# Two graph layers on one core: first scores behind the plain block, weight sums in an order of their own, three token tiles lent out

## Chip, cores, metric

One core of one Trainium2 chip. The metric is the device time of one execution of the whole kernel, in microseconds (us); a run gives one number, and the median of several runs is compared. TensorE is PE in the profile (its weight load PEld), VectorE is DVE, ScalarE is ACT, GpSimd is POOL, SyncE is SP.

## What is computed

The input x is 128 graphs of 64 nodes with 768 features, with an adjacency matrix for each graph. x is normalised and passed through relu, and goes through two layers of the following; the result is added to x.

```
m_left  = h @ W_left.T                     # 768 x 768
m_right = h @ W_right.T
u = (h m_left.T) on and above the diagonal, (h m_right.T) below it, / sqrt(768)
attention = exp(u) * adj, each row divided by its sum
h = relu(layer_norm(attention @ (h @ W_lin.T + b)))
```

## The kernel before

Layers are numbered l = 0 and 1 in the code (layer one is l = 0). Each layer has a first pass (pass_one: the scores and the attention) and a second pass (pass_two: the rest). Tokens are cut into 32 parts of 256 (4 graphs each), each a tile "ht" of 128 x (6 x 256). The work below is that of pass_one.

**Products.** For a part, m_left and m_right together are 2 x 3 x 3 blocks of 256 x 256 x 256, so 18 weight blocks ("raw", values 0 to 17). They are not multiplied one by one, but by a fast scheme: 40 products (PRODUCTS), each of one *weight form* and one *token form*, serve three parts at once. Weight forms are sums of raw blocks, made once a layer: W_OPS lists 101 sums (values 18 to 118), 50 of them without a factor other than 1 on the first operand; only those can go to POOL, the others go to DVE. Token forms are sums of the nine token blocks of three parts: T_OPS lists 38 (values 9 to 46), made anew for each block of three parts, on POOL, always in the order of T_OPS. READS says to which of the 18 outputs each product is added: the first addition to an output is a copy on ACT, the others are adds on DVE, from PSUM into the tiles M.

**Order.** `put(slot, f)` writes work into a plan; `turn_of(slot)` runs what stands there, two slots a product. Each engine works its own queue in order, so the slot fixes only the order of what each queue gets. Layer one begins with a **plain block** (`order`, L877 on): parts 0 and 1 by the 18 raw blocks, 12 chains of 3 products each, 36 products or 72 slots; each chain's bank is copied into M by ACT (L889). So there is time to make weight sums. Then `for k in ...` goes over blocks of three parts with 40 products each: k = 1 begins at slot 72 and k = 2 at slot 152. The **scores** of block k-1 (`scores`, L733, small matmuls of tokens by M) stand behind product 3 of block k, and the softmax of these scores (`chain`, wm on POOL first, L745) is put 10 slots behind the start of the block.

**Weight sums.** `Weights` holds which value lies in which of 51 tiles g (REG). `some(eng, reach)` (L531) takes the first of the next 10 (POOL: 40) sums whose operands are there, DVE preferring those with a factor. On DVE an operand is copied by ACT into a PSUM bank first (`stage`, L517) and read from there. `turn_of` counts 0.62 us a DVE sum and 1.35 us a POOL sum against the slot's time, plus the time of what `timed` marks on DVE; ScalarE's work is not counted. POOL gets weight sums in slots 8 to 59. `need(v)` gives out a sum, on DVE, if a product needs it and it isn't there yet.

**Token sums.** `Tokens.step` gives one to POOL if the parts are ready (`ready`), if fewer than 11 token tiles are out (LIMIT) and if a tile is free; it takes the one that has been free longest.

**Preparing parts.** `prepare(b, slot)` makes parts 2b and 2b+1 from rows of x, one step a slot: four statistics on DVE (L336), one square root on ACT and the scales on DVE, four norms on ACT (L412), four transposes on DVE (L465), the store to DRAM (L461, SP). Three slots later SP loads the part in its new layout (L368), and 16 slots after that it counts as ready. The rows of the next block are asked for at the end of this one (behind block 2: 8 slots later, slot 53). Block 1 is prepared from slot 16, block 2 from 30 and block 3 from 60. Blocks 1 and 2 give parts 2 to 5; k = 1 uses parts 2, 3 and 4.

## Time and profile before

| | us |
|---|---|
| median of 3 runs | 2648.96 (2647.83 to 2654.08) |
| the profiled execution | 2648.42 |
| its span, first to last instruction | 2646.6 |
| TensorE busy | 2591.6 |
| VectorE busy | 1780.6 |
| GpSimd busy | 1763.1 |
| ScalarE busy | 935.4 |

A row of a timeline gives the start of a group of instructions from the span's start, its length, the engine, the line in the kernel, the operation, out<-in by the program's names, shapes and the count; in brackets stands how long the engine had been idle before, and what ended that. Where a helper issues the instruction its line is the helper's: L245 is every add of two tiles, L522 an add with a factor. A float32 matmul appears as two, so a product has 8 and a chain 24.

### The profile page before, as it was taken

Reading aid. Unit: us, or ns where it says so; the run is one execution under the profiler, and the core shown is the slowest. Engines: PE = TensorE matmul, PEld = TensorE weight load, DVE = VectorE, ACT = ScalarE, POOL = GpSimd, SP = SyncE. Lnnn points to the kernel's source line nnn. Section 1 sums busy time; section 2 is a strip of 40 time slices with the busy share of each in tenths; the row PEclk is TensorE's granted clock in tenths of the full one; section 3 lists DMA queues with packets and bytes.
Section 4 is the critical chain, followed back from the end, with each engine's and each line's share of the span. In section 5 each row is a group of like instructions: output and inputs, shape, how many; then the busy total and the mean of one; then the engine's idle time right before and its main releaser. Section 6 shows DMA issues by size and latency. Waiting matters only on the chain. (4 is left out here: it accounts for less than half of the span.)

```text
span 2646.6 us, 47202 instructions
## 1 busy us (share of the span) xinstructions
PE 2591.6 (98%) x18122; PEld 2217.1 (84%) x18122; DVE 1780.6 (67%) x2888; ACT 935.4 (35%) x1969; POOL 1763.1 (67%) x1392
## 2 busy tenths in 40 slices
PE   9899999999999999999999999999999989999998
PEld 8788888888888888888798888888888878887886
DVE  7878787777768445554456667677666676666667
ACT  5522223223113244454542222122222335555453
POOL 4766676666668657676276666667666657878786
PEclk9999999999999999999999999999999999999999
DMA  7443534343421354445794424253532215555655
GB/s 220 113 111 86 124 93 110 93 119 79 98 60 56 123 156 149 159 139 182 219 282 101 121 68 108 71 129 93 136 98 70 67 49 157 157 167 166 177 161 146
DMA packets 258465, 331.84 MB, mean 125 GB/s; under 512 B 56002, under 2 KB 190402, under 8 KB 258242
## 3 DMA queue, kind: packets, MB, share of 16 engines
q1 hardware_dynamic: 241442, 320.56, 44.3%
q10 hardware_dynamic: 16800, 8.26, 1.2%
q8 instruction: 145, 2.38, 0.4%
q14 instruction: 78, 0.64, 0.1%
HBM read 213.39 MB, written 115.34 MB: 124 GB/s over the span
## 5 line engine op out<-in xcount | busy, mean ns | idle before, releaser
L245 POOL TENSOR_TENSOR g<-ht 128x512 f32<-128x512 f32 (+1 forms) x620 | 785.9, 1279 | 420.8 <-PE Z L702 71.6
L245 POOL TENSOR_TENSOR g<-g,g 128x512 f32<-128x512 f32 (+1 forms) x310 | 397.9, 1291 | 136.7 <-PE C L702 22.0
L245 POOL TENSOR_TENSOR g<-ht,g 128x512 f32<-128x512 f32 (+1 forms) x272 | 346.1, 1282 | 164.8 <-PE Z L702 42.8
L702 PE MATMUL X<-g,g 128*128 128x256 f32 (+1 forms) x1080 | 252.9, 377 | 6.0 <-DVE m L914 6.0
L1006 PE MATMUL Z<-g,g 128*128 128x256 f32 x1024 | 244.1, 380 | 3.5 <-ACT hl L300 3.2
L702 PE MATMUL C<-g,g 128*128 128x256 f32 x1008 | 239.7, 381 | 4.9 <-POOL g L245 2.2
L702 PEld LDWEIGHTS X<-g,g 128*128 128x128 f32 x1080 | 203.0, 191 | 34.8 <-DVE m L914 6.8
L702 PE MATMUL Y<-g,g 128*128 128x256 f32 (+1 forms) x968 | 225.7, 376 | 3.8 <-POOL g L245 3.8
L1006 PEld LDWEIGHTS Z<-g,g 128*128 128x128 f32 x1024 | 191.6, 190 | 35.8 <-issue 4.1
L379 ACT ACTIVATE ht<-ht,b_col,a_col 128x256 f32<-128x256 f32 x384 | 196.1, 591 | 69.0 <-DMA ht<-h 53.8
L702 PEld LDWEIGHTS C<-g,g 128*128 128x128 f32 x1008 | 190.5, 190 | 32.9 <-POOL g L245 3.5
L702 PE MATMUL Z<-g,g 128*128 128x256 f32 (+1 forms) x936 | 217.0, 375 | 0.0
L702 PE MATMUL D<-g,g 128*128 128x256 f32 x880 | 209.8, 381 | 1.8 <-POOL g L245 1.8
L702 PEld LDWEIGHTS Y<-g,g 128*128 128x128 f32 x968 | 182.0, 190 | 27.8 <-POOL g L245 4.2
L702 PE MATMUL V<-g,g 128*128 128x256 f32 (+1 forms) x840 | 194.6, 375 | 3.1 <-POOL g L245 1.6
L702 PEld LDWEIGHTS Z<-g,g 128*128 128x128 f32 x936 | 174.5, 190 | 23.1
L702 PEld LDWEIGHTS D<-g,g 128*128 128x128 f32 x880 | 168.1, 191 | 25.7 <-POOL g L245 2.5
L1006 PE MATMUL X<-g,g 128*128 128x256 f32 x768 | 182.7, 379 | 0.0
L702 PEld LDWEIGHTS V<-g,g 128*128 128x128 f32 x840 | 157.6, 191 | 23.3 <-POOL g L245 1.7
L1206 POOL TENSOR_TENSOR z<-z,b 128x768 f32<-128x768 f32 x62 | 112.7, 1829 | 81.7 <-DVE z L1203 77.2
L245 DVE TENSOR_TENSOR m<-m,Y 128x512 f32<-128x512 f32 (+2 forms) x196 | 126.5, 667 | 58.4 <-ACT m L910 35.7
L245 DVE TENSOR_TENSOR m<-m,D 128x512 f32<-128x512 f32 x180 | 118.2, 677 | 70.0 <-ACT m L910 51.3
(222 smaller groups left out, 4612.0 us busy)
## 6 DMA issues: line engine op xcount, KB each, us to landing
ht<-h SPq DMA_DIRECT2D x126, 768.0 KB, 6.3
h<-xb SPq DMA_DIRECT2D x124, 384.0 KB, 6.6
z<-z SPq DMA_DIRECT2D x128, 192.0 KB, 3.1
x<-z SPq DMA_DIRECT2D x128, 192.0 KB, 5.4
xr<-in_x_dram SPq DMA_DIRECT2D x120, 192.0 KB, 3.8
out_dram<-xr SPq DMA_DIRECT2D x120, 192.0 KB, 2.7
x<-in_x_dram SPq DMA_DIRECT2D x112, 192.0 KB, 5.4
g<-form SPq DMA_DIRECT2D x40, 256.0 KB, 5.6
```

The source lines that it names most:

```text
L245: (eng.tensor_add if sign == "+" else eng.tensor_sub)(o, a, b)
L379: nc.scalar.activation(ht, ht, AF.Relu, bias=cols[1][:, c:c + 1], scale=cols[0][:, c:c + 1])
L702: nc.tensor.matmul(o, w[:, c, g * P:(g + 1) * P], t, start=(new and g == c == at == 0), stop=(c == K2 - 1), skip_group_check=True)
L1006: nc.tensor.matmul(p[:, n], b[t][:, c, r * P:(r + 1) * P], w[s][:, c, :], start=(i in FIRST and i not in PRELOAD and n == c == 0), stop=(c ...
L1206: nc.gpsimd.tensor_add(zs[k], zs[k], rows["b"])
```

## The change

- **Scores.** In layer one the scores of parts 0 and 1 stand directly behind the plain block, ahead of product 0 of block 1; the products are then read one by one from the first on. Their softmax is put 2 slots behind the start of the block in place of 10.
- **Weight sums.** They are given out from a list of their own, START_OPS. `turn_of` keeps clocks for VectorE, ScalarE and GpSimd, which also count norms, copies and the wait of the scales. `some` works out when each of the next 10 (POOL: 20) sums could begin, by its operands, its tile and its engine, and takes the first that could begin within 0.7 us of the earliest. VectorE may be given work up to 0.5 us ahead (behind slot 72: 3.5 us). POOL gets sums from slot 0 to 59. The bank of the scores is no staging bank from chain 10 on; two staging banks stay in use in block 1.
- **Tiles.** A tile is chosen by the time at which its last planned use ends, for weight sums and for token sums. While weight sums are left, 9 token tiles may be out, and from slot 60 on a weight sum leaves one tile free. Part 5's place lends three tiles to token sums that are dead by product 20, and the places of parts 0 and 1 lend six more behind their scores; all go back at slot 113, when parts 5, 6 and 7 are loaded.
- **Slots.** Block 1 is prepared from slot 19, block 2 from 31; block 3's parts count as ready 16 slots behind the load in place of 22.

The numbers of matmuls, token sums, weight sums and reads stay as they are.

```diff
+    clock = {"vector": 0.0, "scalar": 0.0, "pool": 0.0}
-    def timed(us, f):
-        f.vector = us
+    def timed(f, *steps):
+        f.steps = steps
         return f
+    def passes(f):
+        for e, us in getattr(f, "steps", ()):
+            clock[e] += us
...
+    START_OPS = (
+        4, 27, 14, 0, 3, 2, 1, 9, 29, 6, 7, 12, 26, 15, 36, 8, 80, 10, 30, 11, 83, 81, 68, 5, 16, 56, 31, 39, 85,
...
     class Weights:
         def take(self):
             of = max(self.extra, free, key=len)
-            return of.popleft() if of else None
+            if not of:
+                return None
+            t = min(of, key=lambda t: busy.get(id(t), 0))
+            of.remove(t)
+            return t
+        def begins(self, eng, op):
+            dead = self.dead(op)
+            t = self.at[dead] if dead is not None else min(self.extra or free or (None,), key=lambda t: busy.get(id(t), 0))
+            x, y = (self.made.get(s, 0) for s in (op[1], op[3]))
+            at = max(y, self.until.get(id(t), 0), clock[NAMES[eng]])
+            if self.stage and eng is nc.vector:
+                x = max(x, clock["scalar"], self.until.get(id(self.stage[0]), 0)) + 0.6
+            return max(x, at)
         def emit(self, eng, op):
+            if dead is None and len(free) <= self.spare:
+                return False
+            us = 1.3 if eng is nc.gpsimd or not self.stage else 0.65
+            end = clock[NAMES[eng]] = self.made[v] = at + us
...
+        def some(self, eng, reach, now):
+            ops = [(max(self.begins(eng, op), now) + (0.4 if eng is nc.vector and op[2] == 1 else 0), n, op)
+                   for n, op in enumerate(self.left[:reach])
+                   if op[1] in self.at and op[3] in self.at and (eng is nc.vector or op[2] == 1)
+                   and (len(free) > self.spare or self.dead(op) is not None)]
+            if not ops:
+                return False
+            soon = min(ops)[0] + 0.7
+            at, _, op = next(o for o in ops if o[0] <= soon)
+            return at <= now + 4.5 and self.emit(eng, op)
...
     class Tokens:
         def emit(self, eng):
             v, a, b, sign = self.queue.pop(0)
-            t = free.popleft()
-            self.out += 1
+            if self.own and self.last[v] < SOON:
+                t = self.own.popleft()
+            else:
+                t = min(free, key=lambda t: busy.get(id(t), 0))
+                free.remove(t)
+                self.out += 1
...
     def pass_one(l, start, final):
-            weights, tokens = Weights(() if l else W_OPS, 2, True), TOKENS[l]
+            weights, tokens = Weights([] if l else [W_OPS[i] for i in START_OPS], 2, True), TOKENS[l]
             def turn_of(slot):
+                now = slot * 0.87 if l == 0 or slot >= 80 else slot * 0.6 + 20.8
+                if slot == start["tokens"]:
+                    weights.spare = 1
+                for e in clock:
+                    clock[e] = max(clock[e], now - 0.5)
...
-                    while clock["vector"] <= now and weights.some(nc.vector):
-                        clock["vector"] += 0.62
+                    while clock["vector"] <= now + (3.5 if slot > 2 * PLAIN else 0.5) and weights.some(nc.vector, 10, now):
+                        pass
+                    if slot < start["tokens"]:
+                        while clock["pool"] <= now + 0.5 and weights.some(nc.gpsimd, 20, now):
+                            pass
+                tokens.limit = Tokens.LIMIT - 2 * bool(weights.left)
+            def lend(*ps):
+                views = [HT[1, 0, p][:, j * K2:(j + 1) * K2, :] for p in ps for j in range(3)]
+                tokens.own.extend(views)
+                tokens.mine.update(id(t) for t in views)
+            if l == 0:
+                for p in range(2, 6):
+                    HT[1, 0, p] = big.tile([P, C, TH], F32, name="ht", bufs=6)
+                lend(5)
+                def back():
+                    assert len(tokens.own) == 9
+                    tokens.own.clear()
+                    load_part(1, 0, 5)
+                put(begins(1) + 2 * SOON + 1, back)
...
-                    lag = 22 if b > 2 else 30 if l else 16
+                    lag = 22 if b > 3 - l else 30 if l and b < 3 else 16
+                    if l == 0 and 5 <= p < 8:
+                        at = begins(1) + 2 * SOON + p - 4
...
+                if n == 10:
+                    weights.stage = [KEEP["Z"], KEEP["V"]]
...
-            weights.stage = []
+            weights.stage = [] if l else [KEEP["Z"], KEEP["V"]]
+            if not l:
+                scores(0)
+                lend(0, 1)
...
-                    put_all(slot + 2 * SCORED + 4, softmax(k - 1), 3)
+                    put_all(slot + (2 * SCORED + 4 if l or k > 1 else 2), softmax(k - 1), 3)
...
-                    if i == SCORED and k:
+                    if i == SCORED and l + k > 1:
                         scores(k - 1)
-                    if i >= SCORED or k == 0:
+                    if i >= SCORED or l + k < 2:
...
-    pass_one(0, {"weights": 0, "pool": 8, "tokens": 60, 1: 16, 2: 30}, final_of(0))
+    pass_one(0, {"weights": 0, "tokens": 60, 1: 19, 2: 31}, final_of(0))
```

More of the change, by code (lines that the diff above doesn't have):

```diff
@@ L474, in places @@
             pool.tile(shape, F32, name=n, bufs=bufs)
+    busy = {}
+    NAMES = {nc.vector: "vector", nc.gpsimd: "pool"}
     class Weights:
@@ L491, in __init__ @@
             self.extra = deque(extra)
+            self.made, self.until, self.spare = {}, busy, 0
         def used(self, v):
@@ L509, in emit @@
                 return False
+            us = 1.3 if eng is nc.gpsimd or not self.stage else 0.65
+            end = clock[NAMES[eng]] = self.made[v] = at + us
+            if self.stage and eng is nc.vector:
+                bank = self.stage.pop(0)
+                self.stage.append(bank)
+                clock["scalar"] = max(self.made.get(a, 0), clock["scalar"], self.until.get(id(bank), 0)) + 0.6
+                self.until[id(bank)] = end
+                bank = bank.rearrange("p (c d) -> p c d", c=K2)
+                nc.scalar.copy(bank, x)
+                x = bank
+            for s in (a, b):
+                self.until[id(self.at[s])] = max(self.until.get(id(self.at[s]), 0), end)
+            self.until[id(t)] = end
             if dead is not None:
@@ L592, in __init__ @@
             self.count = {}
+            first = {t: i for i, (_, t) in reversed(list(enumerate(PRODUCTS)))}
+            for v, a, b, _ in reversed(T_OPS):
+                for s in (a, b):
+                    first[s] = min(first.get(s, 99), first[v])
+            self.last = {v: max([i for i, (_, t) in enumerate(PRODUCTS) if t == v] +
+                                [first[o] for o, *ab, _ in T_OPS if v in ab]) for v, *_ in T_OPS}
+            self.own, self.mine, self.limit = deque(), set(), self.LIMIT
         def value(self, k, v, cut=False):
@@ L610, in step @@
         def step(self, slot, eng=None):
-            if self.k >= len(SUPER) or slot < self.ready.get(self.k, 10 ** 9) or self.out >= self.LIMIT or not free:
+            if self.k >= len(SUPER) or slot < self.ready.get(self.k, 10 ** 9) or self.out >= self.limit or not free:
                 return False
@@ L631, in used @@
             if v >= 9 and n == self.uses[v]:
-                free.append(self.at.pop((k, v)))
-                self.out -= 1
+                t = self.at.pop((k, v))
+                (self.own if id(t) in self.mine else free).append(t)
+                self.out -= id(t) not in self.mine
         def need(self, k, v):
```

58 lines of the change are left out of this document (30 added, 28 removed), and 3 rows, old and new, of the table START_OPS.

## The prediction

> **What bounds the kernel now.** I read the page's busy times first, then the busy time by stretch, then TensorE's instructions in order of time, and then the queue of each engine that releases them.
>
> ```profile
> span 2646.6 us, 47202 instructions
> PE 2591.6 (98%) x18122; PEld 2217.1 (84%) x18122; DVE 1780.6 (67%) x2888; ACT 935.4 (35%) x1969; POOL 1763.1 (67%) x1392
> ```
>
> TensorE is busy for 2591.6 of 2646.6 us. The change takes no matmul away, so it can win only idle or slow TensorE time, and 55.0 us of idle time are left in the whole span. By stretches of 25 us the only large hole of the first 150 us is here (columns: PE, PEld, DVE, ACT, POOL busy, granted clock, DMA share, GB/s):
>
> ```profile
> 75.00:100.00 25.00, 16.29 (x226) 12.98 (x227) 20.44 (x35) 14.97 (x28) 19.34 (x17) 0.80 0.49 124
> 80.00:85.00 5.00, 3.61 (x9) 2.90 (x10) 4.79 (x9) 4.95 (x10) 3.18 (x3) 0.50 1.03 200
> ```
>
> TensorE's rows show that this is the seam between the plain block and layer one's first 40 products (start, length, what; in brackets the idle time before):
>
> ```profile
> 17.75 5.35 PE L702 MATMUL D<-ht,g 128*128 128x256 f32 x24
> ...
> 69.55 5.34 PE L702 MATMUL Y<-ht,g 128*128 128x256 f32 x24
> 77.08 2.51 PE L702 MATMUL C<-g,g 128*128 128x256 f32 x8 [2.19 <-POOL g L245]
> 81.39 3.78 PE L702 MATMUL D<-g,g 128*128 128x256 f32 x8 [1.79 <-POOL g L245]
> 84.96 2.03 PE L702 MATMUL X<-g,g 128*128 128x256 f32 x8
> 90.80 2.57 PE L702 MATMUL Y<-g,g 128*128 128x256 f32 x8 [3.80 <-POOL g L245]
> 93.30 5.16 PE L733 MATMUL sc<-m,ht 128*32 128x95 f32 x192
> 99.49 1.97 PE L702 MATMUL C<-g,g 128*128 128x256 f32 x8 [1.04 <-ACT m L910]
> 101.30 1.89 PE L702 MATMUL D<-g,g 128*128 128x256 f32 x8
> ...
> 160.00 1.89 PE L702 MATMUL Y<-g,g 128*128 128x256 f32 x8
> 168.73 4.60 PE L733 MATMUL sc<-m,ht 128*32 128x95 f32 x211
> ```
>
> The ten chains from 17.75 to 69.55 lie 5.18 us apart, so the plain block would be over at 74.73. From product 5 (101.30; I count from 0) to product 39 (160.00) are 34 products, 1.7265 us each, without a gap: after the seam nothing waits. The later scores need 4.60/211 = 21.8 ns a matmul, so 192 cost 4.19 us; at 93.30 they took 5.16. Without any wait and at full clock product 4 would start at 74.73 + 4 x 1.7265 + 4.19 = 85.83. It started at 99.49. **The seam costs 13.66 us**, and that is what can be won. Every wait but the last names POOL, so I looked at POOL's queue, and at those behind it.
>
> ```profile
> 69.47 6.33 POOL L245 TENSOR_TENSOR g<-g,g 128x512 f32<-128x512 f32 x5 [5.95 <-ACT Z L517]
> 75.76 2.50 POOL L245 TENSOR_TENSOR g<-ht 128x512 f32<-128x512 f32 x2
> 78.72 1.27 POOL L245 TENSOR_TENSOR g<-ht 128x512 f32<-128x512 f32 x1 [0.45 <-DMA ht<-h]
> 83.09 2.51 POOL L245 TENSOR_TENSOR g<-ht 128x512 f32<-128x512 f32 x2 [1.75 <-DVE g L522]
> 88.13 2.61 POOL L245 TENSOR_TENSOR g<-ht,g 128x512 f32<-128x512 f32 x2 [2.53 <-DVE g L522]
> 97.26 1.43 POOL L745 TENSOR_TENSOR wm<-adj,tri 128x256 f32<-128x256 f32 x2
> 108.51 1.28 POOL L245 TENSOR_TENSOR g<-g,g 128x512 f32<-128x512 f32 x1 [0.52 <-PE C L702]
> ```
>
> Token sums are given in the fixed order of T_OPS. Values 9 and 10 run at 75.76, value 11 waits for token part 4 until 78.72, 13 and 15 wait for DVE to let go of a tile, and 16, which product 3 needs, ends at 90.74: product 3 starts at 90.80. So tokens set the seam, for three reasons: weight sums ahead of them on POOL, part 4 by DMA, and tiles that other sums still hold. Part 4's rows come from block 2's chain:
>
> ```profile
> 49.01 1.00 DVE L336 BATCH_NORM_STATS2 st<-m 128x6 f32<-128x384 f32 x2
> 57.04 0.69 DVE L522 SCALAR_TENSOR_TENSOR g<-sc,g 128x512 f32<-128x512 f32 x1 [2.56 <-ACT sc L517]
> 61.05 3.55 DVE L465 STREAM_TRANSPOSE xb<-m 128x768 f32<-128x768 f32 x4
> 83.52 0.68 DVE L522 SCALAR_TENSOR_TENSOR g<-sc,g 128x512 f32<-128x512 f32 x1
> 84.12 0.68 DVE L245 TENSOR_TENSOR g<-Z,g 128x512 f32<-128x512 f32 x1
> 91.21 1.01 DVE L336 BATCH_NORM_STATS2 st<-x 128x6 f32<-128x384 f32 x2
> 94.11 0.81 DVE L245 TENSOR_TENSOR g<-g,g 128x512 f32<-128x512 f32 x1
> ```
>
> ```profile
> 64.62 5.17 SPq L461 DMA_DIRECT2D h<-xb  x4
> 70.98 4.88 SPq L368 DMA_DIRECT2D ht<-h  x2
> 75.96 6.56 SPq L361 DMA_DIRECT2D x<-in_x_dram  x8
> ```
>
> Slot s of the plain block lies at 17.75 + 0.8633 (s - 6) = 12.57 + 0.8633 s. Block 2's first statistics are given out in slot 31, that is 39.3, and run at 49.01: DVE is 9.7 us behind the order written for it, because that order counts DVE's sums but not ScalarE's copies and norms, for which DVE waits (57.04).
>
> **The change part by part.** *Scores moved.* The 192 matmuls are the same; in place of 93.30 they stand at 74.73 and cover 4.19 us in which POOL and DVE go on. They read the last chains' copies in M: those of token part 0 first, so the first half (2.1 us) needs chain 10's copy and the second half, from 76.8, chain 11's. The softmax of these scores moves from slot 82 to 74: POOL's 1.43 us for wm now lie among the token sums that decide.
>
> *Token sums.* By T_OPS and PRODUCTS, products 0, 1, 3, 5, 7, 9, 11 need 1, 4, 8, 11, 15, 17, 20 token sums, then hardly more than one a product. With scores first product 0 is due at 78.92 and product 11 at 78.92 + 11 x 1.7265 = 97.91. Twenty sums of 1.28 us and wm are 27.0 us, so the first must start by 70.9, and part 4 must be in by 97.91 - 18 x 1.28 - 1.43 = 73.4. After the change POOL gets no weight sum from slot 60 on and token sums from slot 65 (68.7). Block 2 starts a slot later, in slot 32 (40.2); if DVE keeps to its order and block 2 takes as long as before from statistics to the end of its transposes (49.01 to 64.60, 15.6), these end at 55.8, and value 11 can read part 4 as long after them as before (78.72 - 64.60 = 14.1), at 69.9: 3.5 us to spare. The lent places (three at once, six behind the scores) remove the waits for DVE at 83.09 and 88.13; the six are free at 78.9, when value 15 or so is due. Cost of the token part: 0, against the full 13.66 before.
>
> *Weight sums in their own order.* The closure of product 5 is 28 sums of 101, but in the new order the sum for product 2 stands 72nd, so about 72 must be there by 82.4. Before, 101 were done but for the 13 from 83.52 to 94.11: 88 by 83.5. So 72 leave room, 16 x 0.60 us (83.52 to 84.12) on DVE, against block 3's statistics (some 4.7 us), which now come before the seam. The 29 left run among the products' reads, where DVE has this much room (PE, PEld, DVE, ...):
>
> ```profile
> 115.00:130.00 15.00, 15.00 (x71) 13.16 (x70) 12.61 (x25) 1.57 (x3) 7.93 (x7) 1.00 0.66 146
> 130.00:145.00 15.00, 15.00 (x71) 13.21 (x70) 11.83 (x26) 2.18 (x3) 10.85 (x10) 1.00 0.69 205
> ```
>
> Some 19% of 69 us are 13 us, and 29 x 0.60 are 17.4, of which POOL can take those without a factor. That is tight, but a bank is read again only four products later (5.2 us of slack): I take 0, at worst the missing 4.4.
>
> *What is late next: block 3's rows.* Its first statistics stand in slot 61 (65.2), and DVE now reaches them in time. Before, they ran at 91.21, so no row shows when their data came.
>
> ```profile
> x<-in_x_dram SPq DMA_DIRECT2D x32, 192.0 KB, 5.8
> ```
>
> SP issues the rows behind block 2's store and part 4's load: 75.96 - 64.62 = 11.3 after the store, less the dropped half of the load (2.4), so from 55.8 + 8.9 = 64.7. Eight issues take 6.56; the fourth goes at 67.2 and the eighth at 70.4, and 5.8 later are 73.0 and 76.2. So DVE stands from 65.2 to 73.0, again until 76.2, and ends the last two statistics (2.4) at 78.6. Queued behind them: DVE's sums; on ScalarE the square root of slot 69, and behind that chain 11's copy (slot 70, some 0.6 us), done at about 79.5. The second half of the scores waits for it, 79.5 - 76.8 = **2.7 us**. The sums given out from slot 69 to product 2 (slot 76) are at most 6.0 us of work and the 3.5 us that the new order may run ahead, so done between at once and 88.4, while product 2 is due at 85.1: 0 to 3.3 us; I take **1.5**, near the middle, since no row is nearer to one end. Below nothing is possible for neither: the bare chain of matmuls is the floor.
>
> *The rest.* The token tile is the least recently planned, not the oldest freed; parts 5 to 7 load in slots 113 to 115 for a block that is due at slot 152; block 3's lag is 6 slots shorter: 0, hidden by POOL's lead (rivals).
>
> *The clock.* After gaps of 2.19 and 1.79 us the stretch 80 to 85 was granted 0.50, and product 1 took 3.78 us. A wait of 2.7 us could so cost up to 1.7 us more; I take 0, since the matmuls before it run without a gap, and keep 1.7 for the range. The Trainium skill ("TensorE: Matmul & The Clock Gate", Part 1: The HAM clock gate) says that the clock is halved after an idle window of about 3.4 us; by it a wait of 2.7 us costs nothing more. The row here shows the half clock behind shorter gaps, so trace and rule agree only if several gaps add up.
>
> *Sum.* 2648.42 (the profiled execution; 1.82 lie around its span) - 13.66 + 2.7 + 1.5 = 2638.96. That execution lies 0.54 below the median of 2648.96, so **2639.5** against the median: 9.5 us, 0.36%.
>
> **The rivals.** *Tokens stay late.* The new clocks count no DMA. If part 4 and the tiles come as before, the 28th value ends where it did (108.51 + 1.28 = 109.8) and product 11 follows; before it started at 101.30 + 6 x 1.7265 = 111.66. The gain is 1.9 us: 2647. For it: POOL's chain of waits; against it: the 9.7 us that block 2 gains. The same price has a change that doesn't do what it says, where sums not yet given out are forced in just before their product, behind the reads of the last one.
>
> *Block 3's rows later still.* DVE's stand is then on the path microsecond for microsecond: rows 4 us later give 2643.5. For it: SP issues them last.
>
> *Slower: tiles in the later blocks.* Tokens.emit now picks by planned time, so in the 20 later blocks of products a sum may write into the tile that the last product still reads while an older one is free, and start up to one product (1.73 us) late.
>
> ```profile
> PE V L702 <- POOL g L245: 1.6, 1, 1.6
> 320.61 1.28 POOL L245 TENSOR_TENSOR g<-ht,g 128x512 f32<-128x512 f32 x1 [0.52 <-PE D L702]
> ```
>
> If each of 20 loses 1.73, it is 34.5: 2674. It decides from (9.5 + 7.9)/1.73, ten blocks. Against it: POOL there already waits for each product in turn, so one tile is free at a time and there is nothing to pick; TensorE felt such a wait only once behind the first block (1.6 us).
>
> **How the numbers follow.** About 0.3% (7.9 us) is what a measurement of this kernel can tell from no change. My forecast has 0.57, tokens late 0.16, rows later 0.15, tiles 0.12. So faster 0.57, same 0.31, slower 0.12. The range goes down to 2648.42 - 13.66, less 0.8 for the spread of runs, 2634.0, and up over the rows and the late tokens to 2648.0.
>
> **What would show it.** Right: sc at 74.7 ahead of the products, the first token sum by 70.9 and value 11 no later than 73.4, block 2's transposes over by 56, DVE idle for DMA x before 79, product 4 at about 90. Wrong: token sums that wait for DMA ht or DVE g behind 79; DVE's last reads of M behind TensorE by more than four products; new waits for POOL behind 160.

## The result, and the profile after

The kernel after takes 2665.27 us (median of 6 runs, 2659.61 to 2670.83), the kernel before on the same chip 2650.38 (6 runs): ratio 1.0057 [1.0046, 1.0067], so 14.9 us slower, where 9.5 us faster was forecast. The profiled execution took 2662.88 us.

The page of the kernel after (busy time, share of the span, instructions):

```profile
span 2661.1 us, 47149 instructions
PE 2593.5 (97%) x18122; PEld 2217.5 (83%) x18122; DVE 1788.0 (67%) x2885; ACT 937.1 (35%) x1974; POOL 1768.1 (66%) x1395
```

TensorE is busy 1.9 us longer, and the span is 14.5 us longer: the rest, 12.6 us, is new idle time. TensorE's instructions in order of time show where the first of it lies (start, length, what; in brackets the idle time before and its releaser):

```profile
11.78 5.42 PE L777 MATMUL C<-ht,g 128*128 128x256 f32 x24 [0.70 <-ACT x L428]
...
75.42 0.86 PE L808 MATMUL sc<-m,ht 128*32 128x95 f32 x32
77.06 2.17 PE L808 MATMUL sc<-m,ht 128*32 128x95 f32 x96 [0.78 <-ACT m L994]
81.41 2.22 PE L808 MATMUL sc<-m,ht 128*32 128x95 f32 x64 [2.18 <-ACT m L994]
83.56 2.92 PE L777 MATMUL C<-ht,g 128*128 128x256 f32 x8
...
91.49 1.89 PE L777 MATMUL C<-ht,g 128*128 128x256 f32 x8
...
107.21 1.97 PE L777 MATMUL Y<-ht,g 128*128 128x256 f32 x8 [1.27 <-DVE m L259]
...
124.30 1.97 PE L777 MATMUL Y<-ht,g 128*128 128x256 f32 x8 [0.28 <-DVE m L1024]
129.74 3.68 PE L777 MATMUL C<-g,g 128*128 128x256 f32 x8 [3.48 <-POOL g L259]
134.89 2.00 PE L777 MATMUL D<-g,g 128*128 128x256 f32 x8 [1.47 <-POOL g L259]
138.35 2.00 PE L777 MATMUL X<-g,g 128*128 128x256 f32 x8 [1.47 <-POOL g L259]
...
167.84 1.89 PE L777 MATMUL Y<-g,g 128*128 128x256 f32 x8
...
176.56 4.61 PE L808 MATMUL sc<-m,ht 128*32 128x95 f32 x214
```

Product 4 starts at 91.49 against 99.49: 8.0 us are won at the seam, as the change means to. But product 39 starts at 167.84 against 160.00. From product 4 to product 39 it is 76.35 us in place of 60.51: **15.8 us are lost** inside the same block: 3.6 by product 11 (107.21 against 111.66; products 6 and 7 wait 0.58 each for token sums, product 11 waits 1.27 for VectorE's reads), 3.3 more by product 19, which starts at 124.30, and 8.9 from there to product 22 (138.35), where the brackets name POOL. Part of the 8.9 is the clock: product 20 takes 3.68 us in place of some 1.9, and from 129.70 to 133.50 the granted clock was 0.55, behind a gap of 3.48.

The second loss is in the later blocks. The scores of block 1 start 7.8 us late (176.56 against 168.73), those of block 10 17.7 us late; the first of layer two are 15.5 us late, and from there to the end the distance hardly changes. So layer one's blocks 2 to 10 lose another **9.9 us**. TensorE's score rows of block 10 and of layer two's first block, before and then after:

```profile
860.36 3.59 PE L733 MATMUL sc<-m,ht 128*32 128x95 f32 x137 [1.14 <-DVE m L245]
...
1399.42 4.13 PE L733 MATMUL sc<-m,ht 128*32 128x95 f32 x192
```

```profile
878.08 6.15 PE L808 MATMUL sc<-m,ht 128*32 128x95 f32 x252 [1.15 <-DVE m L259]
...
1414.94 4.13 PE L808 MATMUL sc<-m,ht 128*32 128x95 f32 x192
```

TensorE's waits from 165 to 930 us in the kernel after (total us, times, longest). The kernel before has no wait for POOL in this window:

```profile
PE V L777 <- POOL g L259: 2.2, 2, 1.1
PE Y L777 <- POOL g L259: 1.1, 1, 1.1
PE D L777 <- POOL g L259: 1.1, 1, 1.1
```

Now the queue that stands behind the first loss. POOL in the kernel after:

```profile
75.54 2.52 POOL L259 TENSOR_TENSOR ht<-ht 128x512 f32<-128x512 f32 x2
80.42 1.27 POOL L259 TENSOR_TENSOR g<-ht 128x512 f32<-128x512 f32 x1 [2.37 <-DMA ht<-h]
...
120.11 1.28 POOL L259 TENSOR_TENSOR g<-ht,g 128x512 f32<-128x512 f32 x1 [8.77 <-DVE g L259]
...
128.42 1.27 POOL L259 TENSOR_TENSOR g<-ht,g 128x512 f32<-128x512 f32 x1 [5.67 <-DVE g L259]
133.57 1.26 POOL L259 TENSOR_TENSOR g<-ht 128x512 f32<-128x512 f32 x1 [3.88 <-PE C L777]
137.03 2.49 POOL L259 TENSOR_TENSOR g<-g,g 128x512 f32<-128x512 f32 x2 [2.20 <-PE D L777]
```

Two token sums wait 8.77 and 5.67 us for a tile that a VectorE sum still uses. VectorE in the kernel after:

```profile
31.23 0.68 DVE L259 TENSOR_TENSOR g<-sc,g 128x512 f32<-128x512 f32 x1
...
37.33 0.18 DVE L416 RECIPROCAL rs<-sd 128x4 f32<-128x4 f32 x1 [0.36 <-ACT sd L413]
37.54 4.96 DVE L422 SCALAR_TENSOR_TENSOR nb<-mv,rs 128x4 f32<-128x4 f32 x1
44.99 0.69 DVE L578 SCALAR_TENSOR_TENSOR g<-Z,g 128x512 f32<-128x512 f32 x1 [2.49 <-ACT Z L567]
...
54.34 0.16 DVE L422 SCALAR_TENSOR_TENSOR nb<-mv,rs 128x4 f32<-128x4 f32 x1
60.11 3.56 DVE L490 STREAM_TRANSPOSE xb<-m 128x768 f32<-128x768 f32 x4 [5.60 <-DMA h<-xb]
63.59 0.65 DVE L578 SCALAR_TENSOR_TENSOR g<-V,g 128x512 f32<-128x512 f32 x1
...
83.47 1.02 DVE L350 BATCH_NORM_STATS2 st<-x 128x6 f32<-128x384 f32 x2
...
88.25 0.69 DVE L259 TENSOR_TENSOR g<-V,g 128x512 f32<-128x512 f32 x1 [3.52 <-POOL wm L820]
...
119.32 0.65 DVE L259 TENSOR_TENSOR g<-V,g 128x512 f32<-128x512 f32 x1
...
127.66 0.68 DVE L259 TENSOR_TENSOR g<-V,g 128x512 f32<-128x512 f32 x1
```

Read the chain backwards. Product 20 (129.74) waits for the token sum of 128.42; that waits for the weight sum of 127.66 to let go of its tile; and that weight sum is one of 28 that VectorE still makes after 83.5, the last at 155.50. Why so many? The program gives them out so: VectorE makes 72 weight sums in layer one, and the kernel below that leaves out those given out behind the plain block makes 43, so 29 stand behind it (one of them runs before 83.5). Ahead of it VectorE has little room: between 31.23 and 63.59 it makes one weight sum (44.99), where the kernel before makes 10 between 35 and 63. In that time it has block 1's and block 2's norms to do and stands for 4.96 us in an instruction of four columns (0.16 the next time), for 2.49 us for ScalarE, and for 5.60 us for the store that still reads xb, of which there is one place. Counted from the rows, 44 weight sums are made on VectorE before 83.5 where the kernel before makes 62.

VectorE also stands idle where it is short of time: 3.52 us ahead of 88.25. The bracket names POOL, but ScalarE's copy for this sum (V) starts at 87.54 and takes 0.61, so the sum could not start before 88.15. The copy stands behind the first reads of product 0, for which ScalarE waited 4.21 us. In the profile named next the same wait is 2.69 us, and the bracket names ScalarE.

**How much of this is one execution.** The first kernel of the experiments differs from the kernel after only in the token sums of later blocks; the plain block is the same program. In its profile the instruction of 4.96 us takes 1.25, and the scores wait for no copy:

```profile
37.09 1.25 DVE L422 SCALAR_TENSOR_TENSOR nb<-mv,rs 128x4 f32<-128x4 f32 x1
```

```profile
86.98 1.89 PE L777 MATMUL C<-ht,g 128*128 128x256 f32 x8
```

Its product 4 (the second row) starts 12.5 us ahead of the kernel before, and products 4 to 39 take 79.4 us. So 8.0 and 15.8 are the split of one execution, 12.5 and 18.9 that of another; the scores of block 1 start 7.8 and 6.4 us late. It too has made 44 weight sums by 83.5, so the 28 that are left do not come from the 4.96 us.

The busy time from 100 to 125 (columns as in the prediction) shows the price:

```profile
100.00:125.00 25.00, 21.58 (x94) 16.93 (x93) 22.26 (x38) 13.95 (x22) 13.82 (x11) 1.00 0.14 27
```

VectorE is 89% busy while TensorE and POOL have holes.

### The profile page after: what moved, and what is told of

Read it like the earlier page. It is cut to its first block, busy times and chain, and to the rows that moved or that the text cites. A ratio compares the mean times of both kernels' runs of the same rounds, so it can differ in the third digit from the quotient of the medians.

```text
span 2661.1 us, 47149 instructions
## 1 busy us (share of the span) xinstructions
PE 2593.5 (97%) x18122; PEld 2217.5 (83%) x18122; DVE 1788.0 (67%) x2885; ACT 937.1 (35%) x1974; POOL 1768.1 (66%) x1395
## 5 line engine op out<-in xcount | busy, mean ns | idle before, releaser
L259 POOL TENSOR_TENSOR g<-g,g 128x512 f32<-128x512 f32 (+1 forms) x300 | 381.6, 1283 | 118.7 <-DVE g L578 24.8
L777 PE MATMUL X<-g,g 128*128 128x256 f32 (+1 forms) x1056 | 246.1, 376 | 7.1 <-DVE m L1024 5.6
L777 PEld LDWEIGHTS X<-g,g 128*128 128x128 f32 x1056 | 197.3, 190 | 35.0 <-DVE m L1024 6.7
L777 PE MATMUL Y<-g,g 128*128 128x256 f32 (+1 forms) x928 | 215.7, 376 | 1.1 <-POOL g L259 1.1
L777 PE MATMUL D<-g,g 128*128 128x256 f32 x856 | 202.6, 380 | 2.9 <-POOL g L259 2.9
L777 PEld LDWEIGHTS Y<-g,g 128*128 128x128 f32 x928 | 174.5, 190 | 23.7 <-POOL g L259 1.5
L777 PEld LDWEIGHTS D<-g,g 128*128 128x128 f32 x856 | 162.5, 190 | 26.2 <-POOL g L259 4.4
L259 DVE TENSOR_TENSOR hl<-hl,Y 128x512 f32<-128x512 f32 (+1 forms) x136 | 89.0, 655 | 113.0 <-PE Y L1116 97.0
```

Source lines behind the costliest of these rows:

```text
L259: (eng.tensor_add if sign == "+" else eng.tensor_sub)(o, a, b)
L777: nc.tensor.matmul(o, w[:, c, g * P:(g + 1) * P], t, start=(new and g == c == at == 0), stop=(c == K2 - 1), skip_group_check=True)
```

## The experiments

My theory after the result was: the later loss is the choice of the token tile; the loss in block 1 is VectorE, which has more to do there than time, and the tiles are only the place where this shows. The rival for block 1: an order or a tile that makes one product wait for the last, so that no work need be taken away. Every ratio below is against the kernel before on the same chip. The products are counted from 0.

### Which tile a token sum takes

The first kernel lets token sums of blocks 2 to 10 and of layer two take again the tile that has been free longest; the second does so everywhere.

```diff
-                t = min(free, key=lambda t: busy.get(id(t), 0))
+                t = free[0] if self.l or self.k > 1 else min(free, key=lambda t: busy.get(id(t), 0))
                 free.remove(t)
```

> The changed kernel, but from block 2 of layer one on (and in layer two) a token sum takes the tile that has been free longest, as before the change; block 1 keeps the choice by planned time. Theory: the changed kernel loses 9.9 us between the scores of block 1 (7.8 us behind the kernel before) and those of block 9 (17.7 us behind) because the choice by planned time writes into the tile that the last product is still reading. Then this kernel is 9 to 10 us below the changed one, about 2655 us, and the 1.1 us waits of TensorE for POOL behind the scores are gone. Rival: those blocks are late for another reason (VectorE's reads behind schedule from block 1 on); then it stays at about 2665 us.

Measured: 1.0017 [1.0008, 1.0026], median 2656.64; TensorE has no wait for POOL left from 165 to 930 us. Against 1.0057 that is 0.40%, some 10.6 us: by the ratios the later blocks' loss was this choice; in the trace about half of it is gone.

```diff
-                t = min(free, key=lambda t: busy.get(id(t), 0))
-                free.remove(t)
+                t = free.popleft()
```

> The changed kernel, but every token sum takes the tile that has been free longest, in block 1 too. Theory: products 20 to 22 of block 1 (5.4, 3.5 and 1.8 us apart from their followers, some 9 us lost) wait because one tile, the one with the lowest planned time, is used for one token sum after the other; then a further 9 us go beside those of the later blocks, about 2646 us. Rival: no other tile is free there, because weight sums not yet used hold them; then products 20 to 22 stay as they are, and it comes out like the kernel with the choice changed in the later blocks only, about 2655 us.

Measured: 1.0006 [0.9996, 1.0016], median 2654.37: some 3 us more, not 9, and the intervals of the two overlap. POOL in this kernel:

```profile
116.12 1.28 POOL L259 TENSOR_TENSOR g<-ht,g 128x512 f32<-128x512 f32 x1 [10.19 <-DVE g L259]
...
124.43 1.27 POOL L259 TENSOR_TENSOR g<-ht,g 128x512 f32<-128x512 f32 x1 [5.68 <-DVE g L259]
128.02 1.27 POOL L259 TENSOR_TENSOR g<-ht 128x512 f32<-128x512 f32 x1 [2.32 <-DVE g L578]
```

The waits for a product (3.88 <-PE C and 2.20 <-PE D above) are gone, and the two long ones for VectorE are not. Products 4 to 39 take 75.5 us. So one tile handed to and fro was at most the small part of the block's loss.

The counter-test is the kernel before with a poor choice in layer one's blocks 2 to 10, the free tile with the lowest number:

```diff
-            t = free.popleft()
+            t = min(free, key=lambda t: next(n for n, r in enumerate(REG) if r is t)) if self.l == 0 and self.k > 1 else free[0]
+            free.remove(t)
```

> The kernel before, with nothing changed but the place of a token sum in the blocks from 2 on of layer one: of the free tiles the one with the lowest number, in place of the one that has been free longest. Theory: any fixed order of preference picks tiles just let go, POOL waits for the product that still reads them and its lead shrinks; 9 blocks of about 1 us make 5 to 10 us, 2657 to 2662 us. Rival: only one tile is ever free there, so the choice doesn't matter; 2652 us, level.

Measured: 1.0038 [1.0025, 1.0050], median 2660.70, some 10 us slower. The largest of TensorE's waits for POOL behind 190 us (1.6 in the kernel before), and its scores of block 10 (860.36 in the kernel before):

```profile
PE V L703 <- POOL g L245: 3.7, 3, 1.5
```

```profile
873.10 6.53 PE L734 MATMUL sc<-m,ht 128*32 128x95 f32 x265 [1.14 <-DVE m L245]
```

So in the kernel before, a poor choice of tile alone makes a loss as large as that of the later blocks.

### The move by itself

The first kernel is the kernel after with the scores back behind product 3; the second is the kernel before with nothing but the move.

```diff
-            if not l:
-                scores(0)
-                lend(0, 1)
...
-                    if i == SCORED and l + k > 1:
+                    if i == SCORED and k:
                         scores(k - 1)
+                        if l + k < 2:
+                            lend(0, 1)
```

> The changed kernel with the scores of parts 0 and 1 back behind product 3 of block 1, their softmax 10 slots behind the block's start and the first reads behind them; the six places of parts 0 and 1 are lent from there. Theory: the move wins some 8 us at the seam (product 4 starts at 91.5 in place of 99.5) and costs nothing elsewhere; then this is about 8 us above the changed kernel, 2673 us. Rival: the move is what crowds VectorE behind the seam (softmax, reads and the weight sums left over come together), so products 4 to 22 lose less without it, and it is level with the changed kernel or below, 2655 to 2665 us.

Measured: 1.0069 [1.0055, 1.0082], median 2669.41: the move is worth some 3 us in the kernel after, not 8, and the intervals overlap. Products 4 to 39 take 75.6 us without it too, so it is not the move that crowds block 1.

```diff
             weights.stage = []
+            if not l:
+                scores(0)
...
-                    if i == SCORED and k:
+                    if i == SCORED and l + k > 1:
```

> The kernel before, with nothing changed but the scores of parts 0 and 1: directly behind the plain block, the softmax 2 slots behind, reads from the first product on. Theory: ScalarE gives the last chain's copy only at 87.9 us there, so the scores can't end before about 91 us, and the gain is what four products need less of waiting: 0 to 2 us, 2648 to 2650. Rival: the scores cover 4.2 us of the waiting for token sums whatever the copies do: 2646 us.

Measured: 1.0028 [1.0018, 1.0039], median 2660.17: 7.4 us slower, which neither theory had. TensorE, ScalarE and VectorE of this kernel:

```profile
93.39 5.68 PE L733 MATMUL sc<-m,ht 128*32 128x95 f32 x192 [18.04 <-DVE g L245]
```

```profile
91.50 0.58 ACT L889 COPY m<-Y 128x512 f32<-128x512 f32 x1
```

```profile
92.65 0.68 DVE L245 TENSOR_TENSOR g<-sc,g 128x512 f32<-128x512 f32 x1
```

The scores need the last chain's copy, which stands in ScalarE's queue behind the copies for weight sums and ends at 92.08, and their bank sc, which is a staging bank until VectorE has read it, at 93.33. TensorE stands for 18 us, and products 0 to 3, which needed neither, stand behind the scores. By itself the move loses. The other parts of the change take sc out of staging and let ScalarE's copies come in time.

### What fills block 1

All of these stand on the second kernel above (tile free longest everywhere; 1.0006). First two that leave out work: the weight sums that are left when the products begin, and the 66 adds on VectorE that read block 1's products.

```diff
                 lend(0, 1)
+                weights.skip = True
...
+            if self.skip:
+                pass
```

> The changed kernel with the oldest free tile for every token sum, and without the 29 weight sums that are not yet given out when the plain block ends: their copies on ScalarE and their sums on VectorE are left out (so block 1 and all later blocks of layer one multiply by tiles that hold other values). Theory: these sums, given to VectorE between the reads of block 1's products, are the loss of 15 us between products 4 and 39 (75.5 us there against 60.4 before); without them products 4 to 39 take 60 to 62 us and the whole 2637 to 2640 us. Rival: the loss is that of the token sums (places, POOL's waits for TensorE), not of weight sums; then it stays at 70 us and more, and the whole at 2650 us and above.

Measured: 0.9974 [0.9964, 0.9984], median 2644.79; products 4 to 39 take 63.95 us, and POOL waits for VectorE nowhere between 84 and 132 us. The whole is 5 us above what the theory asked.

```diff
+                        elif l + k == 1:
+                            pass
                         elif abs(c) == 1:
```

> The changed kernel with the oldest free tile for every token sum, and without VectorE's 66 reads of block 1's products (the first read of each output, on ScalarE, stays; so the scores of block 1 are wrong). The weight sums stay where they are. Theory: VectorE is crowded behind the seam, so with 40 us of reads gone it catches up, lets go of the tiles in time, and products 4 to 39 take 60 to 63 us, the whole some 2637 to 2640 us. Rival: the sums are late by their order and their tiles, not for want of VectorE's time; then products 19 to 22 still wait some 7 us and the whole stays above 2645 us.

Measured: 0.9957 [0.9940, 0.9974], median 2640.98; products 4 to 39 take 62.5 us, and product 20 waits for nothing. The second kernel keeps every weight sum, tile and order and takes only VectorE's time away, and the stall goes: POOL's longest waits for VectorE are 4.31, 0.67 and 0.61 us in place of 10.19, 5.68 and 2.32, and TensorE does not feel them. So with this order and these tiles it is want of VectorE's time that makes the stall; that no other order could avoid it is not shown.

Next, four that move work in time or to another engine. Block 1 prepared earlier, to part it from block 2's transposes:

```diff
-    pass_one(0, {"weights": 0, "tokens": 60, 1: 19, 2: 31}, final_of(0))
+    pass_one(0, {"weights": 0, "tokens": 60, 1: 16, 2: 31}, final_of(0))
```

> The changed kernel with the oldest free tile for every token sum and block 1 prepared from slot 16, as before the change, in place of 19; block 2 stays at 31. Theory: block 2's transposes wait 5.6 us for the store that still reads the one place xb of block 1; with block 1 three slots (2.6 us) earlier that wait shrinks to about 3 us, part 4 and POOL's token sums come 2 to 3 us earlier, and the whole wins 1 to 3 us. Rival: VectorE's time is what lacks; the wait only moves, and 32 in place of 29 sums are left at the seam: level or 1 to 2 us slower.

Measured: 1.0095 [1.0080, 1.0110], median 2677.01: 24 us slower than the kernel it stands on. VectorE's wait for xb shrank as meant, but TensorE now waits for weight sums themselves, up to product 39:

```profile
52.53 3.56 DVE L490 STREAM_TRANSPOSE xb<-m 128x768 f32<-128x768 f32 x4 [2.36 <-DMA h<-xb]
```

```profile
192.03 3.78 PE L776 MATMUL Y<-g,g 128*128 128x256 f32 x8 [6.33 <-DVE g L578]
```

`some` picks by clocks, so other slots gave another order of sums, and sums that products wait for come late. Both theories missed it: with a greedy plan one slot does not change alone.

The softmax of the first scores 24 slots behind the block's start in place of 2:

```diff
-                    put_all(slot + (2 * SCORED + 4 if l or k > 1 else 2), softmax(k - 1), 3)
+                    put_all(slot + (2 * SCORED + 4 if l or k > 1 else 24), softmax(k - 1), 3)
```

> The changed kernel with the oldest free tile for every token sum and the softmax of the first scores 24 slots behind the start of block 1 in place of 2. Theory: of the crowd on VectorE between products 1 and 11 some 5 us (and 1.4 us on POOL) go to slots 96 to 117; if VectorE's lag there is what TensorE feels, products 4 to 19 lose 3 to 5 us less and the whole gains as much. Rival: what is late there are the weight sums still to come, and the work only moves to products 12 to 22, where the token sums already wait: level, within 2 us.

Measured: 0.9998 [0.9988, 1.0009], median 2651.65; products 4 to 39 take 70.7 us in place of 75.5, the whole some 2 us less, with intervals that overlap. Then, on top of it, POOL taking weight sums again from slot 96, and (another kernel) block 4 prepared 16 slots later and block 5 four:

```diff
-                    if slot < start["tokens"]:
+                    if slot < start["tokens"] or slot >= 2 * PLAIN + 24:
```

> The changed kernel with the oldest free tile for every token sum, the first softmax 24 slots behind the start of block 1, and POOL given weight sums again from slot 96 on, when its clock allows. Theory: VectorE has some 80 us of work for the 74 us from the scores to the end of block 1 (29 sums of 0.6, 66 reads of 0.6, two blocks prepared, one softmax), so each sum that POOL takes wins 0.6 us; with five to eight of them products 4 to 39 take 4 to 5 us less than with the softmax moved alone (70.7 us), the whole 2645 to 2648 us, below the kernel before. Rival: POOL's own token sums are the limit there (1.3 us each, one a product), and a weight sum ahead of them delays a product; then it is level or 2 us slower, 2650 to 2654 us.

Measured: 0.9998 [0.9988, 1.0007], median 2650.96: level. POOL took only two weight sums (VectorE makes 70 in place of 72), and its token sums paid for them: TensorE waits for POOL ahead of product 20 for 7.58 us, where the kernel it stands on waits 3.81.

```profile
123.82 3.78 PE L776 MATMUL C<-g,g 128*128 128x256 f32 x8 [7.58 <-POOL g L259]
```

```diff
-                    (b, begins(1, l) + SPACE[l][b > 4][b % 3] + 160 * (b // 3 - 1)) for b in range(3, NB)]:
+                    (b, begins(1, l) + SPACE[l][b > 4][b % 3] + 160 * (b // 3 - 1) + (16 * (b == 4) + 4 * (b == 5)) * (1 - l)) for b in range(3, NB)]:
```

> The changed kernel with the oldest free tile for every token sum, the first softmax 24 slots behind the start of block 1, and block 4's rows prepared 16 slots later, block 5's 4 slots later: block 4's four transposes (3.8 us) leave block 1, its statistics go to its last products. Theory: less work on VectorE in block 1 is time won one to one while it is overloaded; 2 to 4 us, about 2648 us. Rival: the stall sits at products 19 to 23 and is over before block 4's work begins (slot 119, product 23); then it changes nothing, 2651 us.

Measured: 0.9983 [0.9974, 0.9992], median 2646.55: below the kernel before, and by its ratio below the one it stands on, with intervals that just overlap. Its scores of block 1 start at 164.70 against 168.73 before and 167.70 in the kernel it stands on. Of those last 3.0 us, 2.0 are there at product 4 (86.31 against 88.31), ahead of block 4's work, so the trace does not show that the later preparation made them. POOL still waits for VectorE ahead of product 20:

```profile
118.66 1.27 POOL L259 TENSOR_TENSOR g<-ht,g 128x512 f32<-128x512 f32 x1 [7.29 <-DVE g L259]
```

### The instruction of 4.96 us

`nb` (two inputs of four columns) takes 4.96 us where POOL runs sums back to back (14 in the window from 26.46 to 43.82). In eight other kernels with the same program up to there it takes 1.23 to 1.28 us beside the same sums, in one more 4.94. One theory: VectorE and POOL use a path in turn. Rival: the row hides a wait for data. First, on the kernel of 1.0006, ScalarE makes nb, and VectorE only the negative of rs, with one input:

```diff
-                    nc.vector.scalar_tensor_tensor(nb[:, q0:q1], mv[:, q0:q1, 0], -1.0, rs[:, q0:q1],
-                                                   op0=ALU.mult, op1=ALU.mult)
+                    nc.vector.tensor_scalar_mul(nr, rs, -1.0)
+                    for q in range(q0, q1):
+                        nc.scalar.activation(nb[:, q:q + 1], mv[:, q:q + 1, 0], AF.Copy, scale=nr[:, q:q + 1])
```

> The changed kernel with the oldest free tile for every token sum, and the scaled means (nb) of blocks 1 on made on ScalarE (four small activations) in place of one VectorE instruction with two SBUF operands of 128 x 4. That one took 4.96 us in the changed kernel's profile and 1.25 in two others, while POOL ran sums back to back, and 0.16 where POOL was idle. Theory: it waits for POOL to leave the port that both read through; without it VectorE goes on at once, the plain block's end is 1 to 4 us earlier on VectorE, and the spread of the runs (2649.4 to 2660.9) shrinks; 2650 to 2653 us. Rival: it waits for something else (its operands, ScalarE); then the same time is lost one instruction later, and with 1.2 us more on ScalarE it comes out level or 1 us slower.

Measured: 1.0012 [1.0003, 1.0021], median 2654.39: level. The wait moved to the one-input instruction (VectorE), whose only input, made by the instruction before it, is ready at 36.64, so it is not that input that it waits for:

```profile
36.67 4.99 DVE L423 TENSOR_SCALAR nr<-rs 128x4 f32<-128x4 f32 x1
```

Then, on the best kernel so far (0.9983), both steps on ScalarE:

```diff
+                    nc.scalar.activation(nr, rs, AF.Copy, scale=-1.0)
+                    for q in range(q0, q1):
+                        nc.scalar.activation(nb[:, q:q + 1], mv[:, q:q + 1, 0], AF.Copy, scale=nr[:, q:q + 1])
```

> The kernel with the oldest free tile, the softmax later and block 4 later (2646.6 us), and the scaled means of blocks 1 on wholly on ScalarE (five small activations), so that VectorE has no instruction there between the reciprocal and the next sum. Theory: VectorE waits for the port that POOL's sums hold; then the wait of 1.2 to 5.0 us is gone, not moved, VectorE's next sum follows ScalarE's norms, and the kernel is 0 to 2 us faster with less spread (before: 2643.6 to 2651.0): 2645 us. Rival: VectorE stands for another reason; then a wait of that size stands ahead of its next instruction and the time is level or 1 us more.

Measured: 0.9969 [0.9958, 0.9980], median 2647.31 (6 runs). VectorE's next weight sum in the kernel it stands on, where nb took 1.28 us, and then in this one:

```profile
41.14 0.69 DVE L578 SCALAR_TENSOR_TENSOR g<-Z,g 128x512 f32<-128x512 f32 x1 [2.49 <-ACT Z L567]
```

```profile
41.10 0.69 DVE L580 SCALAR_TENSOR_TENSOR g<-Z,g 128x512 f32<-128x512 f32 x1 [3.47 <-ACT Z L569]
```

Nothing stands any more but the 3.47 us for ScalarE, yet the sum comes no sooner than beside the short wait; the step could gain only where the wait is the long one (44.99 in the kernel after). The scores of block 1 start at 168.49, later than in the kernel it stands on (164.70). It is the lowest ratio of the kernels that leave out no work, but its interval overlaps that of the kernel it stands on, and its trace shows no gain: whether this step gains is open.

Last, whether token sums can avoid tiles that VectorE still reads, by taking first those that a product let go of; and both together:

```diff
-                t = free.popleft()
+                t = next((t for t in free if id(t) in let_go), free[0])
+                free.remove(t)
```

> The same kernel (oldest free tile, softmax and block 4 later, 2646.6 us), but a token sum takes first the oldest of the tiles that a product let go, and only without one a tile that weight sums let go. Theory: POOL's waits of 7.3 and 3.1 us for VectorE ahead of products 20 and 21 come from tiles that VectorE, behind its schedule, still uses; with others they go, and products 19 to 22 take 5.2 us in place of 12: 2641 us. Rival: while weight sums are left every tile is in use, and the only free ones are those of weight sums; then nothing changes, 2646 us.

Measured: 0.9999 [0.9989, 1.0009], median 2652.28, by its ratio worse than without. POOL still waits for VectorE, and then (124.41) 3.66 us for a product:

```profile
119.48 1.26 POOL L259 TENSOR_TENSOR g<-ht,g 128x512 f32<-128x512 f32 x1 [7.30 <-DVE g L259]
```

> Both edits together. If both theories hold the gains add, 2639 to 2641 us; if only one does, this is level with that one.

Measured: 0.9988 [0.9979, 0.9996], median 2651.50, between the two. The wait only moved; I take it that every tile is in use there, but no run shows how many are free.

## Why the prediction was wrong

**The seam: near in size, by terms that cancel.** 13.66 less 4.2 is 9.5 us at product 4; 8.0 came in the profiled execution of the kernel after and 12.5 in that of the kernel with the same plain block. Two steps of the working failed: "these end at 55.8" for block 2's transposes, and "69.9" for value 11. They end at 63.67, and it runs at 80.42 (the first token sum at 75.54), because the transposes wait 5.60 us for xb and `nb` costs 4.96; with nb at 1.25 they still end at 59.5. So the rival "tokens stay late" had its condition, but not its price: the scores lie over the time in which the tokens are late, and POOL waits for no tile between 81.7 and 111. Of the two terms, the 1.5 us for product 2's sums was not there: products 1 to 4 follow each other without a gap. The clock, taken as 0, cost 1.8: behind the scores' second wait it was granted 0.65 to 0.67 until 86.40, the last 64 score matmuls took 2.22 us in place of 1.40, and product 1 started 2.75 us behind product 0 in place of 1.73.

**Block 3's rows: right to a microsecond by luck.** I put 2.7 us there. In the kernel after the scores wait 0.78 + 2.18 = 3.0 us, for ScalarE's copies m, but not because of block 3: I misread its slot (here and in the section on the kernel before). For b = 3 the code gives the block's own start, slot 72, and its first statistics run at 83.47, behind the scores. With nb at 1.25 us the scores wait for no copy.

**The 29 weight sums left: the step that failed.** "I take 0, at worst the missing 4.4." It measured 15.8 us, and 18.9 in the other execution. I had set the sums (17.4 us) against VectorE's free share from 115 to 145 of the kernel before, and taken that share for all of the 69 us; but the softmax and the preparation of block 3 lie there for the most part ahead of 115. Counted in the kernel after, from the scores to the end of block 1 VectorE has 29 sums and 66 adds of 0.6 us, a softmax of 6 and two preparations of 8.6 each: 80 us, where 4.2 + 40 x 1.7265 = 73 us were to be had. That is 7 us too much. From 83.5 to 176.5 VectorE is busy for 79.4 us and idle for 13.6 of the 93, 3.52 of them behind ScalarE's copy at 88.25; how the rest of the 15.8 divides is not settled. I took the place where the lack would show to be the banks, which have 5.2 us of slack. It showed most in the tiles: a weight sum late on VectorE holds a tile that POOL needs, POOL works in order, and all later token sums wait with it. The two kernels without the sums and without the adds show that VectorE's time is the cause: 63.95 and 62.5 us in place of 75.5. And the lead that I expected was not there: with POOL's 29 sums 73 were made by 83.5, enough for product 2 as the working asked, but not the 88 of the kernel before.

**The later blocks: the rival that I held at 0.12.** It was priced at up to 1.73 us in each of 20 blocks and argued away by "one tile is free at a time and there is nothing to pick". That is wrong: in layer one there was something to pick, and the choice costs some 10 us there and nothing in layer two. The reason I gave was read from TensorE's waits of the kernel before, where the choice was good; they could not show how many tiles were free. The rows name only 4.4 us of it as waits for POOL; where the other half lies the traces do not tell, and the trace of the kernel without this choice drifts 5.2 us from the scores of block 1 to those of block 10 where after drifts 9.9, though the medians say 10.6.

**The sum.** At the seam -8.0, in block 1 +15.8, in the later blocks +9.9, behind them -3.2: 14.5 us, the difference of the spans. Without the two terms that I put at nothing the sum would be -11.2; no run shows that, and at the -3.2 no experiment looked. Two of the three signs that I had named as wrong came: token sums that wait for DMA ht (2.37) and DVE g (8.77, 5.67) behind 79, and new waits for POOL behind 160. The third tells nothing: VectorE's last reads end 7.5 us behind the end of product 39 in both kernels.

## What to carry to other kernels

When a change leaves work over for the next stretch, add up all that the engine has to do there after the change, instead of reading a free share from another stretch of the trace of before. A late engine shows its price where its buffers are handed on: ask which queue, working in order, will stand behind a tile that it still holds. And when a trace shows no wait for a choice (here of a tile), that says the choice was good, not that there was none. A profile is one execution: here one instruction took 4.96 us in one and 1.25 in another, and product 4 moved by 4.5 us; read two profiles of the same program before you size a term.

## What the runs showed of the hardware

A VectorE instruction of four columns, 0.16 us alone, takes 4.96 us in the kernel after while POOL runs adds of some 1.3 us back to back, about four of them. In one other kernel it takes 4.94, and a TENSOR_SCALAR of one input in its place 4.99; in eight kernels with the same program up to there it takes 1.23 to 1.28 us, about one add. In the three long cases it ends where POOL first leaves a gap between two adds (after: an add ends at 42.47, the next starts at 42.55, and nb ends at 42.50); in short cases (1.28 in the kernel with block 4 later, 1.25 in the one with the oldest tile everywhere) it got through without one. What decides between the two is open. An add with one operand from PSUM goes on beside POOL's (0.68 at 31.23), and so does RECIPROCAL (0.18). With no such instruction in that place VectorE waits only for ScalarE (the row of 41.10). The Trainium skill ("SBUF — State Buffer", SBUF: two separate sides) says that VectorE and GpSimd share one pair of ports by an exclusive lock, taken by a VectorE operation with two SBUF inputs or in a 2-port mode, and that the loser blocks for the whole instruction. The short waits agree in kind; that the loser can wait for some four instructions of the other engine is what the three long ones add. That the lock is the cause was not tried directly.
